# Products with 1/std inside the first projection round, copies on VectorE, and another giving out of the steps between batches

## The chip, the cores and the metric

One core of a Trainium2 chip. The time is device microseconds of one execution of the whole program, the median of three runs of each kernel. One more execution was recorded by the hardware profiler; all durations below come from that one.

## The reference, cut to what matters

Four layers with a residual each act on a field `x` of 4 images, 128 x 128 places, 128 channels, all float32:

```
x = x + L0(gn(x))     # deformable convolution
x = x + L1(gn(x))     # scan over the rows, a 1-d convolution in each step
x = x + L2(gn(x))     # messages
x = x + L3(gn(x))     # triangle multiplication
```

The change concerns the last two. `L2` multiplies every place by `Wself` and adds one term for its row and one for its column. `gn` normalises over groups of 4 channels and all places of an image. `L3` is:

```
xn = layer_norm(x)                                  # over the 128 channels of a place
left  = (xn @ left_w)  * sigmoid(xn @ lgate_w + b)
right = (xn @ right_w) * sigmoid(xn @ rgate_w + b)
out   = einsum('bkjd,bkid->bijd', left, right)      # a 128 x 128 x 128 product per channel
out   = layer_norm(out) * sigmoid(xn @ ogate_w + b)
x     = x + out @ to_out_w + to_out_b
```

## The kernel before, in words

`deform_layer` makes L0, `scan_layer` L1; the field after L1 lies in HBM as `x2T` (channels first). `last_layers` makes L2 and L3 together, batch after batch. It holds one batch at a time in `X`, a tile of 128 channels by 128 x 128 places (64 KB per partition), and one set of projections in `T`, both single. The order of the work is written out by hand: `manual_schedule` keeps, on each of the five engines, the order in which the code emits the instructions, and the parts are Python generators whose steps are interleaved by the loop at L1653. A step is emitted by `step(...)`; `JB` is 8 rows.

For a batch `b` the parts are:

- `messages` (L1333): 16 items. `fetch` loads a tile `x2c` of `x2T` (L1345, SP's queue), POOL adds up the row and column terms (`zc`, L1349); PE multiplies by `ws` (L1363), VectorE adds `zc` and writes `X` transposed (L1368), then takes statistics (L1373). An item is 16 rows by 64 places, so its load has pieces of 64 x 4 = 256 B, and each half of `X` is full after 8 items. The steps of the next batch's messages begin inside the last projection round of the batch before.
- `scaled` (L1379): the group norm's mean and deviation, and eight stores of `X` to HBM as `x3T` (1 MB each, L1394, ACT's queue) for the residual at the end.
- `normed` (L1450): for each of 16 blocks of 8 rows PE centres `X` over the channels into a `pair` of PSUM banks (L1457, two such buffers), ACT squares (L1463), and the centred block is copied back to `X`, by ACT for even blocks (L1468), by VectorE for odd ones (L1470). Every two blocks PE sums the squares (L1491), and a generator `divided` (L1415) takes over: ACT's square root, a trip through HBM (`stdT`) to spread the values over the partitions for a reciprocal, a second trip that loads them spread over all partitions as `rwide` (L1439, two buffers, two loads per block), two products on VectorE (L1446) and a memset of row 0 of `X` to one on POOL (L1447), which carries the bias. Each call of `advance` moves every open `divided` by one step, so a block is multiplied about four double blocks after it was centred, the last ones during the first projection round.
- `multiplied` (L1503), four rounds q = 0 to 3 over 32 of the 128 hidden channels: for each of 16 blocks, 8 matmuls (L1516), a sigmoid on ACT (L1521), two products on VectorE into `T` (L1524), and in every second block an output gate (L1532, L1537, stored to HBM). Then 8 steps of the products over places (L1543, L1547).
- `given_out` (L1553), 40 steps that bring out the batch before: statistics of four columns (L1568), every fourth step their scales with a square root on ACT (L1585), `u` on ACT and POOL (L1632, L1630), transposes (L1602), `y` (L1604, L1605), the residual from `x3T` and the last matmul (L1613, L1617), a copy (L1634) and the store.

The 40 steps are spread over the next batch: 1 ahead of the messages, 3 in them, 4 in `scaled`, 5 in the 25 steps of the norm, 8 in each of the rounds 0 to 2, 3 in round 3. The last batch's steps run alone at the end.

Of the kernel before, what the change touches and what calls it, by code (L numbers as in the profile page):

```python
# [1285 lines left out]
def last_layers(tc, c, terms, w, x2T, out, x3T, gateT, stdT):  # L1286
# [9 lines left out]
    with ExitStack() as ctx:  # L1296
# [36 lines left out]
        def messages(b):  # L1333


            RB, V = 2 * JB, S // 2
            stats = xs[b] = one.tile([P, S // 4, 6], F32, name="stats3")
            todo = [(n, y0) for n in range(2) for y0 in range(0, S, RB)]
            got = []

            def fetch(i):
                if i < len(todo):
                    n, y0 = todo[i]
                    x2c = four.tile([P, RB, V], F32, name="x2c", tag="wide")
                    nc.sync.dma_start(  # L1345
                        x2c, x2T[b, :, y0 : y0 + RB, n * V : (n + 1) * V]
                    )
                    zc = four.tile([P, RB, V], F32, name="zc", tag="wide")
                    nc.gpsimd.tensor_tensor(  # L1349
                        zc, z[:, 0, b, y0 : y0 + RB].unsqueeze(2).to_broadcast([P, RB, V]),  # L1350
                        z[:, 1, b, n * V : (n + 1) * V].unsqueeze(1).to_broadcast([P, RB, V]),
                        ALU.add,
                    )
                    got.append((x2c, zc))

            fetch(0)
            fetch(1)
            yield
            for i, (n, y0) in enumerate(todo):
                x2c, zc = got.pop(0)  # L1360
                pz = pair()
                for h in range(2):
                    nc.tensor.matmul(  # L1363
                        pz[:, h], lhsT=ws[:, b], rhs=x2c[:, JB * h : JB * (h + 1)],
                        start=True, stop=True,
                    )
                x = X[:, n * V : (n + 1) * V]
                nc.vector.tensor_tensor(  # L1368
                    x[:, :, y0 : y0 + RB].rearrange("p w h -> p h w"),
                    pz.rearrange("p n (h w) -> p (n h) w", w=V), zc, ALU.add,  # L1370
                )
                for h in range(2):
                    nc.vector.bn_stats(  # L1373
                        stats[:, 2 * i + h, :], x[:, :, y0 + JB * h : y0 + JB * (h + 1)]
                    )
                fetch(i + 2)
                yield

        def scaled(b):  # L1379

            stats = xs.pop(b)
            mv = two.tile([P, 2], F32, name="mv3")
            nc.vector.bn_aggr(mv, stats.rearrange("p n s -> p (n s)"))
            nc.vector.tensor_tensor(mv[:, 0:1], mv[:, 0:1], w.outb, ALU.subtract)
            mean_ps = single((P, 1))
            nc.tensor.matmul(mean_ps, lhsT=c.gmean, rhs=mv[:, 0:1], start=True, stop=True)
            mean = two.tile([P, 1], F32, name="mean3")
            nc.vector.tensor_copy(mean, mean_ps)
            d = two.tile([P, 1], F32, name="d3")
            nc.vector.tensor_tensor(d, mv[:, 0:1], mean, ALU.subtract)  # L1390
            nc.vector.tensor_tensor(d, d, d, ALU.mult)
            nc.vector.tensor_tensor(d, d, mv[:, 1:2], ALU.add)
            for j0 in range(0, S, 16):
                nc.scalar.dma_start(x3T[b, :, j0 : j0 + 16, :], X[:, j0 : j0 + 16, :])  # L1394
            yield
            var_ps = single((P, 1))
            nc.tensor.matmul(var_ps, lhsT=c.gmean, rhs=d, start=True, stop=True)
            s = two.tile([P, 1], F32, name="s3")
            nc.scalar.activation(s, var_ps, AF.Sqrt, bias=c.eps)
            nc.vector.reciprocal(s, s)  # L1400
            cs = one.tile([P, P], F32, name="cs")
            nc.vector.tensor_scalar(cs, c.center, s, None, ALU.mult)

            shift = two.tile([P, 1], F32, name="shift")
            nc.vector.tensor_tensor(shift, mean, w.outb, ALU.add)
            nc.vector.scalar_tensor_tensor(shift, shift, -1.0, s, ALU.mult, ALU.mult)
            yield
            pc = single((P, 1))
            nc.tensor.matmul(pc, lhsT=c.center, rhs=shift, start=True, stop=True)
            ct = two.tile([P, 1], F32, name="ct")  # L1410
            nc.vector.tensor_copy(ct, pc)
            xs[b] = cs, ct
            yield

        def divided(b, j0, pv):  # L1415

# [11 lines left out]
            nc.vector.reciprocal(rs, rs)  # L1430
            yield
            nc.sync.dma_start(stdT[b, 1, tokens].rearrange("(p e) -> p e", p=P), rs)
            yield
            yield
            for h in range(2):
                rws = []
                for j1 in (j0 + h * JB, j0 + h * JB + 4):
                    rw = two.tile([P, 4 * S], F32, name="rwide")
                    nc.sync.dma_start(  # L1439
                        rw, stdT[b, 1, j1 * S : (j1 + 4) * S].partition_broadcast(P)  # L1440
                    )
                    rws.append((j1, rw))
                yield
                for j1, rw in rws:
                    flat = X[:, j1 : j1 + 4, :].rearrange("p j i -> p (j i)")
                    nc.vector.tensor_tensor(flat, flat, rw, ALU.mult)  # L1446
                nc.gpsimd.memset(X[0:1, j0 + h * JB : j0 + (h + 1) * JB, :], 1.0)  # L1447
            yield

        def normed(b):  # L1450

            cs, ct = xs.pop(b)

            def centred(j1, engine):
                px = pair()
                for n in range(2):
                    nc.tensor.matmul(  # L1457
# [6 lines left out]
                    sq.rearrange("p n e -> p (n e)"), flat, AF.Square, bias=ct  # L1464
                )
                to = X[:, j1 : j1 + JB, :].rearrange("p j i -> p (j i)")
                if engine is nc.scalar:
                    nc.scalar.activation(to, flat, AF.Identity, bias=ct)  # L1468
                else:
                    nc.vector.tensor_scalar(to, flat, ct, None, ALU.add)  # L1470
                return sq

            def advance():
                for d in list(dividing):
                    if next(d, self) is self:
                        dividing.remove(d)

            self = object()
            sqs = [centred(0, nc.scalar)]
            yield  # L1480
            for j0 in range(0, S, 2 * JB):
                sqs.append(centred(j0 + JB, nc.vector))
                advance()
                yield
                if j0 + 2 * JB < S:
                    sqs.append(centred(j0 + 2 * JB, nc.scalar))
                advance()
                yield
                pv = single()
                for q in range(4):  # L1490
                    nc.tensor.matmul(  # L1491
                        pv[32 * q : 32 * q + 32], lhsT=c.mean[:, 0:32],
                        rhs=sqs[q // 2][:, q % 2], start=True, stop=True,
                    )
                del sqs[0:2]
                dividing.append(divided(b, j0, pv))
                advance()
                yield
            while dividing:
                advance()  # L1500
                yield

# [50 lines left out]
        def given_out(b):  # L1553
# [38 lines left out]
            for k in range(-7, NS_ + 1):  # L1592
# [31 lines left out]
                if 0 <= k + 2 < NS_:  # L1624
                    u = us[k + 2] = two.tile([P, 4, P], F32, name="u")
                    for j, (r, m) in enumerate(factors.pop(k + 2)):
                        of = column(b, 4 * (k + 2) + j)
                        to = u[:, j].rearrange("p (q d) -> p q d", q=NQ)
                        if j >= (1 if alone else 4 if k < 6 else 2):
                            nc.gpsimd.tensor_scalar(to, of, r, m, ALU.mult, ALU.add)  # L1630
                        else:
                            nc.scalar.activation(to, of, AF.Identity, bias=m, scale=r)  # L1632
# [8 lines left out]

        order = {getattr(mybir.EngineType, e) for e in ("PE", "Activation", "DVE", "Pool", "SP")}
        ctx.enter_context(tc.manual_schedule(engines=order))
        xs, dividing = {}, []
        END = object()

        def step(of, n=1):
# [4 lines left out]
        out_of = iter(())  # L1652
        for b in range(B):  # L1653

            step(out_of)
            for n, _ in enumerate(msgs):
                if n < 3:
                    step(out_of)
            for n, _ in enumerate(scaled(b)):
                step(out_of, (2, 1, 1)[n])  # L1660
            norm = normed(b)
            for n in range(25):
                step(norm)
                if n in (4, 9, 14, 19, 24):
                    step(out_of)

            msgs = messages(b + 1) if b + 1 < B else iter(())
            for q in range(NQ):
                for n, _ in enumerate(multiplied(b, q)):
                    step(norm)  # L1670
                    if q + 1 < NQ:
                        if n in (1, 3, 5, 7, 9, 11, 15, 20):
                            step(out_of)
                        continue
                    if n in (1, 3, 5):
                        step(out_of)
                    if 7 <= n < 16 or n in (17, 20, 23):
                        step(msgs)
            out_of = given_out(b)
        while step(out_of):  # L1680
# [84 lines left out]
```

## Time and profile before

| | us |
|---|---|
| median of 3 runs (lowest to highest) | 5460.4 (5451.1 to 5470.65) |
| the profiled execution | 5471.3 |
| its span, first to last instruction | 5469.6 |
| PE busy in the span | 4908.4 (90%) |
| DVE busy | 3298.1 (60%) |
| ACT busy | 2491.3 (46%) |
| POOL busy | 1192.2 (22%) |
| `last_layers`, first message item to the end | 3957 to 5470 |
| first q=0 matmul of batches 0 to 3 at | 4082.6, 4402.3, 4758.4, 5113.8 |
| last batch's giving out, alone | 5351 to 5470 |

PE is TensorE's matmuls and PEld its weight loads, DVE is VectorE, ACT ScalarE, POOL GpSimd, SP the engine that issues most DMAs. In a group of the profile the names are `out<-in`, then shapes and the count; then busy time and the mean of one; then the engine's idle time ahead of it and what ended that. A float32 matmul of the code leaves two records.

### The profile page before, as it was taken

To read this page: it belongs to the slowest core of one execution; us is meant where nothing else is said; L and a number is where in the kernel's file an instruction comes from. 1 tells how busy PE (TensorE), PEld (TensorE's weight loads), DVE (VectorE), ACT (ScalarE), POOL (GpSimd) and SP (SyncE) were. 2 spreads that over 40 slices of the span, in tenths; PEclk is the share of its full clock that TensorE was granted. 3 is DMA by queue.
4 is the path that set the end of the run, shared out by engine and by line. 5 is a ranking of instruction groups with operands and counts; after the bars stand their busy time and mean duration, and the time that the engine had idled before them with its cause. 6 is when DMAs were issued, how large, how long until landed. Compare 5 with 4: busy or idle time off the path is not lost. (4 is left out here: it accounts for less than half of the span.)

```text
span 5469.6 us, 162747 instructions
## 1 busy us (share of the span) xinstructions
PE 4908.4 (90%) x68902; PEld 4255.7 (78%) x68902; DVE 3298.1 (60%) x8469; ACT 2491.3 (46%) x5131; POOL 1192.2 (22%) x1097
## 2 busy tenths in 40 slices
PE   1898999999999998989999799999969889798897
PEld 1787788888788787877899799999828478486696
DVE  4676666666566656665555566666654655656545
ACT  1554454544554544544544223323224455563665
POOL 4222121210221201222100011111220233333324
PEclk9999999999998999999999899999989999899998
DMA  5776656665666665655644322222152654646535
GB/s 150 160 160 148 137 133 141 147 151 101 140 139 131 161 120 112 154 121 123 125 91 87 81 82 82 78 78 78 59 156 69 181 169 132 204 152 179 164 130 191
DMA packets 1396696, 710.66 MB, mean 130 GB/s; under 512 B 976717, under 2 KB 1243246, under 8 KB 1386742
## 3 DMA queue, kind: packets, MB, share of 16 engines
q1 hardware_dynamic: 1361810, 625.00, 47.4%
q10 hardware_dynamic: 34148, 75.15, 3.7%
q8 instruction: 545, 8.93, 0.7%
q14 instruction: 193, 1.58, 0.1%
HBM read 417.28 MB, written 282.55 MB: 128 GB/s over the span
## 5 line engine op out<-in xcount | busy, mean ns | idle before, releaser
L606 PE MATMUL conv_ps<-ring,wdef 128*128 128x192 f32 (+2 forms) x7632 | 1297.5, 319 | 8.3 <-DVE x1c L576 5.8
L514 DVE TENSOR_TENSOR m<-t_ps,tent 128x390 f32<-128x390 f32 x1548 | 806.2, 557 | 787.7 <-ACT tent L512 772.2
L606 PEld LDWEIGHTS conv_ps<-ring,wdef 128*128 128x128 f32 x7632 | 1143.3, 195 | 128.0 <-issue 64.8
L512 ACT COPY tent<-t_ps 128x390 f32<-128x390 f32 x1560 | 690.6, 487 | 658.5 <-PE t_ps L498 648.2
L498 PE MATMUL t_ps<-parts_of,spread 57*64 57x99 bf16 (+1 forms) x12384 | 742.6, 275 | 169.8 <-DVE m L514 147.8
L523 PE MATMUL v_ps<-m,pixels 60*64 60x108 f32 (+1 forms) x22704 | 813.8, 264 | 17.6 <-DVE m L514 8.2
L498 PEld LDWEIGHTS <-spread 57*64 57x64 bf16 x12480 | 578.5, 125 | 314.5 <-issue 267.1
L523 PEld LDWEIGHTS v_ps<-m,pixels 60*64 60x64 f32 x22704 | 674.0, 137 | 68.9 <-DVE m L514 22.6
L549 ACT COPY ring<-v_ps 128x432 f32<-128x432 f32 x1032 | 505.0, 525 | 442.6 <-PE v_ps L523 441.9
L420 POOL TENSOR_TENSOR off<-off,koff 72x512 f32<-72x512 f32 x128 | 162.6, 1271 | 1766.8 <-DVE off L417 1766.8
L1516 PEld LDWEIGHTS pair_ps<-wcat,X 128*128 128x128 f32 x4096 | 482.1, 195 | 64.1 <-issue 37.2
L1516 PE MATMUL pair_ps<-wcat,X 128*128 128x128 f32 x4096 | 492.9, 279 | 23.8 <-DVE T L1524 12.3
L1112 PEld LDWEIGHTS own_ps<-diff,wconv 128*128 128x128 f32 x4064 | 494.1, 191 | 13.2
L1524 DVE TENSOR_TENSOR T<-pair_ps,sig 128x256 f32<-128x256 f32 x512 | 280.5, 592 | 370.3 <-ACT sig L1521 370.3
L1112 PE MATMUL own_ps<-diff,wconv 128*128 128x128 f32 x4064 | 494.9, 273 | 0.0
L506 PE MATMUL t_ps<-parts_of,spread 57*64 57x130 bf16 x9288 | 454.9, 225 | 0.6 <-issue 0.6
L1152 POOL TENSOR_TENSOR sum_h<-sum_h,x2c 128x512 f32<-128x512 f32 x128 | 162.7, 1271 | 1142.7 <-DVE x2c L1138 689.7
L438 DVE SCALAR_TENSOR_TENSOR parts<-off,parts 72x512 bf16<-72x512 f32 x384 | 296.1, 772 | 154.0 <-ACT parts L430 148.2
L1068 ACT ACTIVATE rowT<-x1T_ps,t_x,s_x 128x128 f32<-128x128 f32 x512 | 207.4, 566 | 309.9 <-PE x1T_ps L1064 292.5
L506 PEld LDWEIGHTS <-spread 57*64 57x64 bf16 x9312 | 319.5, 108 | 0.6 <-issue 0.5
L1521 ACT ACTIVATE sig<-pair_ps 128x512 f32<-128x512 f32 x256 | 151.2, 597 | 317.1 <-PE pair_ps L1516 201.1
L1101 PE MATMUL both_ps<-carry,wsum 128*128 128x128 f32 x2032 | 269.2, 274 | 1.1 <-DVE carry L1135 1.1
(196 smaller groups left out, 6712.2 us busy)
## 6 DMA issues: line engine op xcount, KB each, us to landing
pixels<-tab SPq DMA_DIRECT2D x688, 123.8 KB
parts_of<-off SPq DMA_DIRECT2D x1032, 55.7 KB
off<-parts SPq DMA_DIRECT2D x64, 891.0 KB
tab<-rows SPq DMA_DIRECT2D x384, 128.0 KB
xin<-in_x_dram SPq DMA_DIRECT2D x128, 256.0 KB
x<-x1c SPq DMA_DIRECT2D x32, 1024.0 KB
x1rows<-x SPq DMA_DIRECT2D x128, 256.0 KB
x2T<-x2c ACTq DMA_DIRECT2D x128, 256.0 KB
```

Source lines behind the costliest of these rows:

```text
L438: nc.vector.scalar_tensor_tensor(parts[:, NSPLIT + i, h : h + RO, 2 : S + 2], off, 0.0, part, ALU.is_gt, ALU.mult,)
L498: nc.tensor.matmul(tp[h : h + HALF, 0, 0:n].rearrange("p (r c) -> p r c", c=PADW)[:, :, i:PADW:RX], lhsT=spread[0:k, kx // 2, i, h : h + H ...
L506: nc.tensor.matmul(tp[h : h + HALF, 1, i * PADW : (i + 1) * PADW], lhsT=spread[HALF : HALF + k, kx // 2, first + i, h : h + HALF], rhs=src ...
L512: nc.scalar.copy(tent[:, 0:n], tp[:, 0, 0:n])
L514: nc.vector.tensor_tensor(m, *pair, ALU.mult)
L523: nc.tensor.matmul(to[p1 : p1 + HALF], lhsT=pix[p0 : p0 + LANES, xb, :], rhs=m[p0 : p0 + LANES, :, RX * xb : RX * xb + w], start=True, sto ...
L549: nc.scalar.copy(to, bodies[side])
L606: nc.tensor.matmul(pc[:, at : at + rows, x0:x1], lhsT=wdef[:, side, k, :], rhs=v[:, :, k if v.shape[2] == NK else kx, x0 + kx : x1 + kx], ...
L1101: nc.tensor.matmul(both, lhsT=wsum[:, j, :], rhs=old[h][:, 1, :, j : j + V], start=(j == 0), stop=(j == NJ - 1),)
L1112: nc.tensor.matmul(own[:, n], lhsT=wt[:, 2 * j + n, :], rhs=diffs[h][:, n, :, j : j + V], start=False, stop=(n == 1 and j == NJ - 1),)
L1516: nc.tensor.matmul(pj[:, j], lhsT=X[:, j0 + j, :], rhs=w.wcat[:, q * 4 * DQ : (q + 1) * 4 * DQ], start=True, stop=True,)
L1524: nc.vector.tensor_tensor(to, pj[:, :, e].rearrange("p j d -> p d j"), sig[:, :, e].rearrange("p j d -> p d j"), ALU.mult,)
```

## The change

Six edits, all in `last_layers`:

1. `messages`: for batch 0 `parts` is 1, so an item is 8 rows by 128 places (pieces of 4 KB). The other batches keep 16 rows by 64.
2. The first half of `X` is stored to `x3T` from SP's queue in step 9 of `messages` for batches 1 to 3; `scaled` stores only the second half there, and the whole for batch 0.
3. `divided` becomes `inverted`, which ends when 1/std is in HBM. The spreading loads and the products are now plain functions, `spread` and `divide`. The loop calls them for block 0 ahead of the first round, and then in the first round, after block n of the projections is emitted: the product of block n+1, then the load for block n+2.
4. All 16 copies of centred blocks are on VectorE.
5. `u` of the first steps of giving out (k < 6) is shared with POOL as in the later ones.
6. The 40 steps are given out anew: 2 in the messages, 5 in `scaled`, 12 in the norm, 7, 7, 6 and 2 in the four rounds. The next batch's messages have 13 steps in round 3 instead of 12.

```diff
@@ messages
-            RB, V = 2 * JB, S // 2
+            parts = 2 if b else 1
+            RB, V = JB * parts, S // parts
+            RH = RB // 2
...
-            todo = [(n, y0) for n in range(2) for y0 in range(0, S, RB)]
+            todo = [(n, y0) for n in range(parts) for y0 in range(0, S, RB)]
...
                 fetch(i + 2)
+                if b and i == len(todo) // 2 + 1:
+                    for j0 in range(0, S // 2, 16):
+                        nc.sync.dma_start(x3T[b, :, j0 : j0 + 16, :], X[:, j0 : j0 + 16, :])
                 yield
@@ scaled
-            for j0 in range(0, S, 16):
+            for j0 in range(S // 2 if b else 0, S, 16):
                 nc.scalar.dma_start(x3T[b, :, j0 : j0 + 16, :], X[:, j0 : j0 + 16, :])
@@ divided -> inverted, spread, divide
             nc.sync.dma_start(stdT[b, 1, tokens].rearrange("(p e) -> p e", p=P), rs)
-            yield
-            yield
-            for h in range(2):
-                rws = []
-                for j1 in (j0 + h * JB, j0 + h * JB + 4):
-                    rw = two.tile([P, 4 * S], F32, name="rwide")
-                    nc.sync.dma_start(
-                        rw, stdT[b, 1, j1 * S : (j1 + 4) * S].partition_broadcast(P)
-                    )
-                    rws.append((j1, rw))
-                yield
-                for j1, rw in rws:
-                    flat = X[:, j1 : j1 + 4, :].rearrange("p j i -> p (j i)")
-                    nc.vector.tensor_tensor(flat, flat, rw, ALU.mult)
-                nc.gpsimd.memset(X[0:1, j0 + h * JB : j0 + (h + 1) * JB, :], 1.0)
-            yield
+
+        def spread(b, j0):
+
+            for j1 in (j0, j0 + 4):
+                rw = two.tile([P, 4 * S], F32, name="rwide")
+                nc.sync.dma_start(rw, stdT[b, 1, j1 * S : (j1 + 4) * S].partition_broadcast(P))
+                spreads.append((j1, rw))
+
+        def divide():
+
+            j0 = spreads[0][0]
+            for j1, rw in spreads:
+                flat = X[:, j1 : j1 + 4, :].rearrange("p j i -> p (j i)")
+                nc.vector.tensor_tensor(flat, flat, rw, ALU.mult)
+            spreads.clear()
+            nc.gpsimd.memset(X[0:1, j0 : j0 + JB, :], 1.0)
@@ normed
-                if engine is nc.scalar:
-                    nc.scalar.activation(to, flat, AF.Identity, bias=ct)
-                else:
-                    nc.vector.tensor_scalar(to, flat, ct, None, ALU.add)
+                nc.vector.tensor_scalar(to, flat, ct, None, ALU.add)
@@ given_out
-                        if j >= (1 if alone else 4 if k < 6 else 2):
+                        if j >= (1 if alone else 2):
@@ the loop over the batches
-            step(out_of)
             for n, _ in enumerate(msgs):
-                if n < 3:
+                if n % 2:
                     step(out_of)
             for n, _ in enumerate(scaled(b)):
-                step(out_of, (2, 1, 1)[n])
+                step(out_of, (2, 2, 1)[n])
             norm = normed(b)
             for n in range(25):
                 step(norm)
-                if n in (4, 9, 14, 19, 24):
+                if n % 2:
                     step(out_of)
+            spread(b, 0)
+            divide()
+            spread(b, JB)
 
             msgs = messages(b + 1) if b + 1 < B else iter(())
             for q in range(NQ):
+                beside = (
+                    (1, 4, 7, 10, 13, 15, 20), (1, 4, 7, 10, 13, 15, 20),
+                    (1, 4, 7, 11, 15, 20), (9, 12),
+                )[q]
                 for n, _ in enumerate(multiplied(b, q)):
-                    step(norm)
-                    if q + 1 < NQ:
-                        if n in (1, 3, 5, 7, 9, 11, 15, 20):
-                            step(out_of)
-                        continue
-                    if n in (1, 3, 5):
+                    if q == 0:
+                        step(norm)
+                        if n + 1 < S // JB:
+                            divide()
+                        if n + 2 < S // JB:
+                            spread(b, (n + 2) * JB)
+                    if n in beside:
                         step(out_of)
-                    if 7 <= n < 16 or n in (17, 20, 23):
+                    if q + 1 == NQ and (7 <= n < 16 or n in (16, 18, 20, 22)):
                         step(msgs)
```

More of the change, by code (lines that the diff above doesn't have):

```diff
@@ L1363, in messages @@
                     nc.tensor.matmul(
-                        pz[:, h], lhsT=ws[:, b], rhs=x2c[:, JB * h : JB * (h + 1)],
+                        pz[:, h], lhsT=ws[:, b], rhs=x2c[:, RH * h : RH * (h + 1)],
                         start=True, stop=True,
@@ L1373, in messages @@
                     nc.vector.bn_stats(
-                        stats[:, 2 * i + h, :], x[:, :, y0 + JB * h : y0 + JB * (h + 1)]
+                        stats[:, 2 * i + h, :], x[:, :, y0 + RH * h : y0 + RH * (h + 1)]
                     )
                 fetch(i + 2)
+                if b and i == len(todo) // 2 + 1:
+                    for j0 in range(0, S // 2, 16):
+                        nc.sync.dma_start(x3T[b, :, j0 : j0 + 16, :], X[:, j0 : j0 + 16, :])
                 yield
@@ L1413, in scaled, with inverted @@
             yield
-        def divided(b, j0, pv):
+        def inverted(b, j0, pv):
             std = three.tile([P, 512], F32, name="std", tag="gate")
@@ L1432, in divided, with centred @@
             nc.sync.dma_start(stdT[b, 1, tokens].rearrange("(p e) -> p e", p=P), rs)
-            yield
-            yield
-            for h in range(2):
-                rws = []
-                for j1 in (j0 + h * JB, j0 + h * JB + 4):
-                    rw = two.tile([P, 4 * S], F32, name="rwide")
-                    nc.sync.dma_start(
-                        rw, stdT[b, 1, j1 * S : (j1 + 4) * S].partition_broadcast(P)
-                    )
-                    rws.append((j1, rw))
-                yield
-                for j1, rw in rws:
-                    flat = X[:, j1 : j1 + 4, :].rearrange("p j i -> p (j i)")
-                    nc.vector.tensor_tensor(flat, flat, rw, ALU.mult)
-                nc.gpsimd.memset(X[0:1, j0 + h * JB : j0 + (h + 1) * JB, :], 1.0)
-            yield
+        def spread(b, j0):
[10 more added lines that the diff above has]
+            nc.gpsimd.memset(X[0:1, j0 : j0 + JB, :], 1.0)
         def normed(b):
             cs, ct = xs.pop(b)
-            def centred(j1, engine):
+            def centred(j1):
                 px = pair()
@@ L1466, in centred @@
                 to = X[:, j1 : j1 + JB, :].rearrange("p j i -> p (j i)")
-                if engine is nc.scalar:
-                    nc.scalar.activation(to, flat, AF.Identity, bias=ct)
-                else:
-                    nc.vector.tensor_scalar(to, flat, ct, None, ALU.add)
+                nc.vector.tensor_scalar(to, flat, ct, None, ALU.add)
                 return sq
             def advance():
-                for d in list(dividing):
+                for d in list(inverting):
                     if next(d, self) is self:
-                        dividing.remove(d)
+                        inverting.remove(d)
             self = object()
-            sqs = [centred(0, nc.scalar)]
+            sqs = [centred(0)]
             yield
             for j0 in range(0, S, 2 * JB):
-                sqs.append(centred(j0 + JB, nc.vector))
+                sqs.append(centred(j0 + JB))
                 advance()
@@ L1485, in normed @@
                 if j0 + 2 * JB < S:
-                    sqs.append(centred(j0 + 2 * JB, nc.scalar))
+                    sqs.append(centred(j0 + 2 * JB))
                 advance()
@@ L1495, in normed @@
                 del sqs[0:2]
-                dividing.append(divided(b, j0, pv))
+                inverting.append(inverted(b, j0, pv))
                 advance()
                 yield
-            while dividing:
+            while inverting:
                 advance()
@@ L1643, in last_layers @@
         ctx.enter_context(tc.manual_schedule(engines=order))
-        xs, dividing = {}, []
+        xs, inverting, spreads = {}, [], []
         END = object()
```

## The prediction, made before the changed kernel ran

> **What bounds the kernel now.** I read the page first, then the busy time by stage, then the groups of instructions, then the timeline of one stage. The change touches only `last_layers`, the last 1,512 us of the span (3957 to 5470 us). In it four batches run one after the other, each through the same stages, so I asked for the busy time of each engine stage by stage. The columns are: stage, its length, busy us (and instructions) of PE, PEld, DVE, ACT, POOL, the granted TensorE clock, the DMA share and GB/s.
>
> ```profile
> core 0: us, PE busy (x) PEld busy (x) DVE busy (x) ACT busy (x) POOL busy (x), PEclk, DMA share, GB/s
> 4039.00:4082.60 43.60, 40.77 (x130) 13.72 (x130) 16.45 (x22) 29.90 (x31) 4.71 (x5) 0.94 0.33 116
> 4082.60:4128.00 45.40, 33.58 (x206) 27.90 (x204) 26.47 (x47) 12.40 (x20) 9.41 (x10) 0.85 0.49 150
> 4147.00:4191.00 44.00, 43.01 (x340) 38.83 (x339) 17.67 (x32) 19.15 (x33) 0.00 (x0) 1.00 0.13 49
> 4299.00:4336.00 37.00, 18.45 (x47) 8.74 (x47) 32.79 (x74) 8.60 (x17) 10.79 (x7) 0.79 0.89 294
> 4336.00:4402.00 66.00, 54.17 (x211) 24.10 (x210) 28.10 (x53) 46.07 (x65) 12.82 (x13) 0.86 0.44 141
> 4402.00:4474.00 72.00, 63.90 (x472) 58.03 (x471) 42.34 (x98) 42.52 (x73) 28.39 (x33) 0.92 0.60 185
> 4474.00:4533.00 59.00, 57.12 (x465) 52.61 (x465) 30.46 (x76) 40.95 (x71) 18.89 (x24) 1.00 0.43 143
> ```
>
> Rows 1 to 3 are batch 0: its norm, most of its first projection round (q=0), and its second (q=1). Rows 4 to 7 are batch 1: the end of its messages with the scales, norm, q=0, q=1. Where PE has nothing to wait for (q=1) it is busy at full clock: a round without giving out takes 44 us, with 8 steps of giving out 59, so a step costs PE (59.1-43.9)/8 = 1.9 us, the price of a step on a full PE. PE has holes in three places: the end of the messages (18 of 37 us busy, DVE 33: DVE bounds it), the norm (54 of 66) and q=0 (64 of 72). Batches 2 and 3 repeat this: norm and q=0 together take 137.1, 134.0 and 135.9 us, from the first matmul of L1457 to the last of L1543. The holes of a batch come to about 40 us; that is all a better order can win in it.
>
> The pieces of a projection round are these groups (mean ns of one before the bar's end):
>
> ```profile
> L1516 PE MATMUL pair_ps<-wcat,X 128*128 128x128 f32 x4096 | 492.9, 279 | 23.8 <-DVE T L1524 12.3 <-POOL X L1447 6.3 <-DVE X L1470 5.1
> L1524 DVE TENSOR_TENSOR T<-pair_ps,sig 128x256 f32<-128x256 f32 x512 | 280.5, 592 | 370.3 <-ACT sig L1521 370.3
> L1521 ACT ACTIVATE sig<-pair_ps 128x512 f32<-128x512 f32 x256 | 151.2, 597 | 317.1 <-PE pair_ps L1516 201.1 <-DVE T L1524 81.2 <-ACT x L1634 30.0
> L1446 DVE TENSOR_TENSOR X<-X,rwide 128x512 f32<-128x512 f32 x128 | 86.7, 695 | 88.3 <-DMA rwide<-stdT 87.8
> L1447 POOL MEMSET X<- 1x1024 f32 x64 | 60.3, 942 | 251.6 <-DVE X L1446 222.8 <-issue 9.9 <-ACT gate L1537 7.2
> ```
>
> The product with 1/std (L1446) waits 88 us for its spread rows, but it runs some blocks ahead of the projections, so most of this is hidden. The timeline of batch 1's q=0 shows the links from one block to the next, and one of batch 0 what a gap does to PE:
>
> ```profile
> 4410.66 0.60 ACT L1521 ACTIVATE sig<-pair_ps 128x512 f32<-128x512 f32 x1 [0.83 <-ACT x L1634]
> 4411.29 1.11 DVE L1524 TENSOR_TENSOR T<-pair_ps,sig 128x256 f32<-128x256 f32 x2 [1.42 <-ACT sig L1521]
> 4412.32 1.37 DVE L1446 TENSOR_TENSOR X<-X,rwide 128x512 f32<-128x512 f32 x2
> ```
>
> ```profile
> 4382.14 1.33 DVE L1446 TENSOR_TENSOR X<-X,rwide 128x512 f32<-128x512 f32 x2 [2.67 <-DMA rwide<-stdT]
> 4383.53 0.94 POOL L1447 MEMSET X<- 1x1024 f32 x1 [3.22 <-DVE X L1446]
> ```
>
> ```profile
> 4089.73 3.49 PEld L1516 LDWEIGHTS pair_ps<-wcat,X 128*128 128x128 f32 x16 [5.31 <-POOL X L1447]
> ```
>
> DVE takes its instructions in the order of the code: the T products of a block (L1524), then the next L1446. A block's 16 matmul records take 1.87 us when blocks follow each other (two in 3.74 us at 4408.63), 2.03 us to the start of its sigmoid, but 3.5 us in the last line, after PE had stood for 5.3 us behind a memset.
>
> **The Trainium skill.** "TensorE: Matmul & The Clock Gate", section "HAM oscillation": gaps of more than about 3.4 us send the array back to half clock. The trace agrees: L1516 records have a median of 275 ns in a full PE and 421 ns after that gap of 5.3 us. "DMA: Bandwidth & Descriptors", "Specifications": pieces under 512 B don't reach line rate. It agrees: x2c (512 KB in pieces of 256 B) lands some 4.4 us after issue with no store beside it, while x3T (1 MB in pieces of 8 KB) lands every 2.5 us. The same page, "Queues, rings and completion order": a DMA engine takes the descriptors of one issuing queue in ring order. The trace has only the case with two queues: an x2c load issued at 3996.8 us, just behind four x3T stores on ACT's queue, landed after 13.9 us.
>
> **The change, part by part** (sums against the profiled execution, 5471.3 us with a span of 5469.6; it lies 10.9 us over the median of 5460.4).
>
> *Products moved into q=0.* In the new loop `divide()` for block n+1 stands after the whole of block n of `multiplied`. On DVE it is therefore behind T(n), which waits for sigmoid(n), which waits for the matmuls of block n; and the matmuls of block n+1 wait for the product and for the memset of row 0. That is a closed chain, once per block: matmuls to sigmoid 2.03 + sigmoid 0.60 + 0.03 + T products up to the next DVE start 1.03 + product 1.33 + 0.06 + memset 0.94 + about 0.05 = **6.07 us**. At half clock the first link is 3.6, and the chain 7.7 us. PE has 1.87 us in it, plus 0.86 for a gate matmul in every second block, plus 2 us where giving out stands. So PE is 40% (batch 0) to 50% full, and some matmuls will run at half clock. I take 6.6 us for batches 1 to 3, where giving out fills six of the gaps, and 7.1 for batch 0, where nothing does. Other work in the gap is hidden: the stats of giving out (1.2 us on DVE) stand behind the product, in the 3.5 us of memset, matmuls and sigmoid; POOL's y and u (2.5 us) stand behind the memset and end before the next. The new spread has two `rwide` buffers for two DMAs, so it starts when the previous product ends; the second lands about 3.0 us after that (batch 0: cycle of 4.05 us per block, of which 1.3 is product), before the 4.7 us that the chain leaves. The square root in `scales` isn't hidden: twice in q=0 ACT does it, u, x and a table load (1.28) ahead of the sigmoid, about 2.25 us late, 4.5 in all. The first spread has nothing ahead of it but the norm: landing, product and memset, 3.5 us.
> Batch 0: 3.5 + 16 x 7.1 + 7.4 (second half of the round, as at 4139.5 to 4146.9) = 124.5 against 64.3 us: **+60**.
> Batches 1 to 3: q=0 is 3.5 + 16 x 6.6 + 4.5 + 7.4 + 2 (one step of giving out there) = 123.
>
> *Norm with twelve steps and DVE copies.* PE per two blocks: 2 x 1.88 + 1.06 + 1.5 steps x 2.05 = 7.9 us, 63 in all. DVE has 16 copies of 1.28 instead of 8 (+10 us) and loses about 11 us of products; ACT loses 8 x 1.11. The copy still waits for the square of the same bank, so a pair buffer is held 1.88 + 1.12 + 1.28 + 0.1 = 4.4 us, 2.2 per block with two buffers; this fits in 7.9 per two. I take 67 us (63 to 72) where 5 steps took 62.5 to 66. Norm and q=0: 190 against 135.7, **+54** per batch. Batch 0 has no giving out; its norm stays at 43.6.
>
> *Giving out taken from elsewhere.* q=1 has 7 steps instead of 8 (-1.9), q=2 6 (-3.5), q=3 none on PE but one item of messages more (-1; batch 3, without messages, -3).
>
> *End of messages, batches 1 to 3.* One item of 3.2 us and two steps' stats fewer on DVE (-5 to -6), scales -3 since PE meets fewer transposes. Against it: four x3T stores (10 us of data) now stand on SP's queue ahead of the last four x2c loads, and hold the next by about 9 us, of which DVE's lag hides some 4. Net **-5** (-9 to +2). POOL's two u for k<6 take load from ACT: nothing, since neither bounds here.
>
> *Batch 0's rows whole.* X is written from 3969.4 to 4032.7, 3.96 us per item; DVE alone needs 1.91 + 2 x 0.685 = 3.2. With 4 KB pieces, and without the x3T stores in the middle, DVE bounds: -12. No row shows the new stride; if it costs, 0. All eight x3T stores now come after the last item, and ACT's square root behind their issue (7.8 instead of 3.1 us): +3. Their data (20 us) runs ahead of the norm's writes.
>
> Sum: batch 0 +60 - 12 + 3 = +51; batches 1 to 3: +54 - 1.9 - 3.5 - 1 - 5 = +43 each, 129; batch 3's last round -2. Together **+178**: 5649 for a profiled run, less 10.9: **5640 us** for the median.
>
> **Rivals.** (1) The chain isn't closed, because products run ahead as before; then q=0 takes PE's own 2.4 (batch 0) to 3.1 us per block. In the sum above the block's time C enters as -252 + 64C, so it turns at C = 3.9 us. 16 x 2.4 + 48 x 3.1 = 187 gives -65: **5395 us**, faster. For it: nothing else in the stage needs more than 3.1 us. Against it: L1446 directly follows L1524 on DVE in the timeline, in code order.
> (2) The spread, not the chain, bounds: SP serves stores of gates, x3 and gate loads in order, and was held 2.3 us at one such place (4409.7 to 4412.0). If each spread came 2.5 us later than I take, the slack of 1.7 is gone and a block costs about 1.4 more: 64 x 1.4 = 90, **5730 us**. Against it: the spread is issued ahead of the step's DMAs.
> (3) Gains and losses cancel, C near 4: **5460 us**.
>
> **How the numbers follow.** Chances: forecast 0.80, rival 1 0.08, rival 2 0.09, rival 3 0.03. Bounds around the forecast: C from 6.07 everywhere (-42) to 7.7 in batch 0 and 7.3 elsewhere (+43); norm -12 to +15; messages -12 to +21 and, in batch 0, up to +12. Taken as independent about 55 either way; I reach a little further down, since half clock is the least certain: **5570 to 5700**. About 0.3% (16 us) is what a measurement of this kernel can tell from no change: faster 0.08, same 0.03, slower 0.89.
>
> **What would show it.** Batch periods of about 398 us instead of 355; L1524 waiting for the sigmoid in every block of q=0; PE's longest idle in the stage ended by POOL's memset; TensorE clock near 0.75 there. Batch 0's messages near 52 us. It is wrong if blocks of q=0 follow in under 4 us, or if L1446 still waits for rwide in most blocks.

## The result, and the profile after

The changed kernel takes **5695.15 us** (median of 4, 5692.24 to 5719.15) against 5455.75 us for the kernel before in the same comparison: ratio **1.0447, 95% interval 1.0408 to 1.0487**, 239 us slower by the medians. The profiled execution has a span of 5692.4 us, against 5469.6.

By the first matmul of the messages, `last_layers` begins at 3952.7 us (before: 3965.4). The code ahead of it is the same in both; from run to run this start moved between 3953 and 3975 us, and the giving out of the last batch at the end took 110 to 121 us without an edit to it. So the stages, not the whole time, are compared below. They are marked by the records of the trace: messages end with the last write of `X`, `scaled` with the first centring matmul, the norm with the last sum of squares, the lead with the first projection, each round with its last product over places. In us:

```
             messages scaled  norm  lead   q=0   q=1   q=2   q=3   batch
before, b=0     67.3    6.2   43.7  -0.1   64.3  43.9  43.9  63.9  333.1
before, b=1     25.3   12.6   62.4   3.4   71.4  59.1  57.6  67.5  359.4
before, b=2     25.3   12.6   59.9   2.6   71.4  59.1  57.6  67.1  355.7
before, b=3     25.3   12.4   60.3   2.2   73.3  59.1  57.6  47.0  337.3
after,  b=0     54.0   10.0   41.3   7.5  126.8  43.9  43.9  67.9  395.1
after,  b=1     26.9   11.1   64.3   7.4  125.2  61.5  52.8  68.1  417.1
after,  b=2     26.4   11.1   64.1   6.7  127.9  59.7  52.8  68.1  416.8
after,  b=3     25.7   11.1   64.3   7.4  125.2  61.4  52.8  43.9  391.8
```

The batches together are 235 us longer, and q=0 alone 225. The busy time by stage of the changed kernel, with the columns as in the prediction, for batch 0's norm, q=0 and q=1, then batch 1's end of messages, scales, norm, lead, the blocks of q=0 and q=1:

```profile
core 0: us, PE busy (x) PEld busy (x) DVE busy (x) ACT busy (x) POOL busy (x), PEclk, DMA share, GB/s
4016.60:4065.40 48.80, 40.62 (x130) 13.52 (x130) 22.97 (x25) 23.87 (x25) 0.94 (x1) 0.92 0.31 112
4065.40:4182.70 117.30, 65.44 (x271) 54.72 (x272) 34.41 (x62) 13.15 (x22) 17.85 (x17) 0.67 0.25 82
4192.00:4236.00 44.00, 43.01 (x340) 38.83 (x339) 17.70 (x32) 19.02 (x32) 0.00 (x0) 1.00 0.13 48
4347.80:4374.70 26.90, 11.51 (x17) 4.47 (x16) 14.77 (x17) 0.59 (x1) 5.71 (x3) 0.75 0.78 221
4374.70:4385.80 11.10, 2.45 (x11) 2.37 (x12) 9.61 (x36) 2.87 (x5) 1.21 (x2) 0.56 0.91 378
4385.80:4450.00 64.20, 61.61 (x321) 34.54 (x320) 39.79 (x94) 49.37 (x77) 28.45 (x36) 0.97 0.42 129
4450.00:4457.40 7.40, 0.05 (x4) 0.00 (x0) 2.02 (x5) 2.29 (x3) 3.28 (x4) 0.81 0.57 173
4457.40:4574.00 116.60, 67.85 (x372) 58.87 (x373) 47.48 (x100) 32.68 (x53) 26.44 (x31) 0.79 0.39 125
4582.60:4644.10 61.50, 57.16 (x451) 52.51 (x450) 28.04 (x68) 37.78 (x65) 16.65 (x21) 0.97 0.38 125
```

The norm is now what one would wish: PE is busy for 61.6 of 64.2 us, with twelve steps of giving out in it. In the blocks of batch 0's q=0 no engine is busy for more than 56% of the time, and the array runs at 0.67 of its clock: that fits a closed chain, though the table alone doesn't show one. PE's 65 busy us there are themselves long because of the clock. The same groups as in the prediction:

```profile
L1518 PE MATMUL pair_ps<-wcat,X 128*128 128x128 f32 x4096 | 562.0, 300 | 240.2 <-POOL X L1453 226.9 <-DVE T L1526 13.2
L1526 DVE TENSOR_TENSOR T<-pair_ps,sig 128x256 f32<-128x256 f32 x512 | 281.0, 591 | 630.3 <-ACT sig L1523 630.3
L1523 ACT ACTIVATE sig<-pair_ps 128x512 f32<-128x512 f32 x256 | 152.7, 597 | 600.1 <-PE pair_ps L1518 499.6 <-DVE T L1526 72.8 <-ACT x L1636 19.9
L1451 DVE TENSOR_TENSOR X<-X,rwide 128x512 f32<-128x512 f32 x128 | 82.1, 681 | 16.9 <-DMA rwide<-stdT 16.9
L1453 POOL MEMSET X<- 1x1024 f32 x64 | 60.3, 942 | 426.4 <-DVE X L1451 426.4
```

Busy times hardly moved, except PE's (493 to 562 us, a record's mean from 279 to 300 ns). The waits did: PE waited 24 us ahead of the projections before, 240 now, 227 of them ended by POOL's memset. The product's own wait for its spread rows fell from 88 to 17. The waits of batch 1's q=0 (who waits, for whom: us in total, times, longest) close the circle. The step from T to the next product isn't among them, since it is no wait but VectorE's own order:

```profile
POOL X L1453 <- DVE X L1451: 88.2, 16, 7.0
ACT sig L1523 <- PE pair_ps L1518: 68.6, 12, 7.7
DVE T L1526 <- ACT sig L1523: 63.7, 15, 5.6
PE pair_ps L1518 <- POOL X L1453: 56.1, 16, 7.4
```

Each of the four waits for the one before it in the chain, in 12 to 16 of the 16 blocks. None of these rows alone is a cause: a reader who stops at the third would blame the sigmoid, at the fourth the memset. In the timeline of batch 0 one turn of the chain reads (lines of other work left out):

```profile
4097.63 0.60 ACT L1523 ACTIVATE sig<-pair_ps 128x512 f32<-128x512 f32 x1 [4.44 <-PE pair_ps L1518]
4098.26 1.07 DVE L1526 TENSOR_TENSOR T<-pair_ps,sig 128x256 f32<-128x256 f32 x2 [4.41 <-ACT sig L1523]
4099.41 1.23 DVE L1451 TENSOR_TENSOR X<-X,rwide 128x512 f32<-128x512 f32 x2
4100.69 0.94 POOL L1453 MEMSET X<- 1x1024 f32 x1 [5.84 <-DVE X L1451]
4101.69 3.78 PE L1518 MATMUL pair_ps<-wcat,X 128*128 128x128 f32 x16 [4.15 <-POOL X L1453]
```

### The profile page after: what moved, and what is told of

Its sections match the earlier page's. It is cut to its first block, busy times and chain, and to the rows that moved or that the text cites. A ratio compares the mean times of both kernels' runs of the same rounds, so it can differ in the third digit from the quotient of the medians.

```text
span 5692.4 us, 162705 instructions
## 1 busy us (share of the span) xinstructions
PE 4957.5 (87%) x68902; PEld 4302.1 (76%) x68902; DVE 3330.4 (59%) x8501; ACT 2434.7 (43%) x5045; POOL 1218.4 (21%) x1145
## 5 line engine op out<-in xcount | busy, mean ns | idle before, releaser
L1518 PEld LDWEIGHTS pair_ps<-wcat,X 128*128 128x128 f32 x4096 | 540.6, 213 | 315.0 <-POOL X L1453 260.0
L1518 PE MATMUL pair_ps<-wcat,X 128*128 128x128 f32 x4096 | 562.0, 300 | 240.2 <-POOL X L1453 226.9
```

The source lines that it names most:

```text
L1518: nc.tensor.matmul(pj[:, j], lhsT=X[:, j0 + j, :], rhs=w.wcat[:, q * 4 * DQ : (q + 1) * 4 * DQ], start=True, stop=True,)
```

## The experiments

Ratios are to the kernel before, run on the same chip as the experiment. "Block" is the mean distance of the 16 blocks of q=0 from first matmul to first matmul, in the profiled execution; a block is called cold where the median of its L1518 records is over 400 ns (it is 421 ns then and 275 in a warm one; over the cold block at 4101.7 us the granted clock was 0.50). In the changed kernel the four batches have blocks of 7.57, 7.35, 7.44 and 7.35 us (6.09 at the shortest), and 14, 8, 9 and 8 cold ones; in the kernel before 3.5 to 3.9 us, and one or two cold ones.

**Products one block further ahead.** Edit to the changed kernel:

```diff
             spread(b, 0)
             divide()
             spread(b, JB)
+            divide()
+            spread(b, 2 * JB)
...
-                        if n + 1 < S // JB:
+                        if n + 2 < S // JB:
                             divide()
-                        if n + 2 < S // JB:
-                            spread(b, (n + 2) * JB)
+                        if n + 3 < S // JB:
+                            spread(b, (n + 3) * JB)
```

> The changed kernel with the products of q=0 one block further ahead: block n+2 is multiplied after block n is projected, so VectorE has the product of block n+1 behind it when it comes to the T products of block n. Closed chain (my theory): the chain is cut; what is left is the product (1.33 us) and its spread with two buffers (3.0 us), 4.35 us a block instead of 7.4 to 7.6. That is 64 x 3 = about -190 us: 5500 us (5470 to 5540). Rival, the spread or SP's queue sets the pace: blocks stay over 6.5 us, 5640 to 5700. Rival, the cost lies in the twelve steps within the norm: unchanged, 5690.

Measured: 5546.47 us, ratio 1.0142 (1.0112 to 1.0173). Blocks of 4.15, 4.85, 4.83 and 4.91 us; q=0 takes 74.8 us in batch 0 and 90 to 93 in the others. PE, VectorE, ACT and POOL have as many instructions as before; what differs is where the products, with their memsets and spreads, stand in the order. Some 160 us came back, less than the 190 expected, since blocks in batches 1 to 3 take 4.8 to 4.9 rather than 4.35. The waits in batch 0's q=0 show that the limit has changed hands:

```profile
DVE X L1451 <- DMA rwide<-stdT: 28.4, 25, 4.4
DVE T L1526 <- ACT sig L1523: 3.2, 3, 1.8
```

VectorE now waits for the spread rows 25 times in its 32 products, and for the sigmoid hardly at all.

**Memset twice.** Edit to the changed kernel:

```diff
-            nc.gpsimd.memset(X[0:1, j0 : j0 + JB, :], 1.0)
+            for _ in range(2):
+                nc.gpsimd.memset(X[0:1, j0 : j0 + JB, :], 1.0)
```

> The changed kernel with the memset of row 0 issued twice for each block of q=0. If the chain is closed and POOL's memset a link of it, each of the 64 blocks grows by one memset (0.94 us and the step to the next instruction): +62 us, ratio 1.056 (1.052 to 1.059), a block at 7.1 us with a warm array and 8.8 with a cold one. If the memset has slack (POOL is 21% busy), the time stays at ratio 1.0447.

Measured: 5784.34 us, ratio 1.0571 (1.0539 to 1.0602). The shortest blocks of batches 1 to 3 are 7.09 us, against 6.09: the whole memset stands in the chain. The means are 8.73 to 8.81 us. In batches 1 to 3, 12 or 13 of 16 blocks are cold, against 8 or 9, so the longer gap also cost clock there. (Batch 0 has 16 cold ones; that says little, since a kernel below with the unchanged loop, the one with the stores behind the last load, has 16 there too.) POOL's 21% of busy time says nothing about the memset's place in the chain.

**Filler matmuls.** Edit to the changed kernel:

```diff
                     if n in beside:
                         step(out_of)
+                    elif q == 0 and n < S // JB:
+                        pf = single()
+                        for j in range(10):
+                            nc.tensor.matmul(
+                                pf[:, 0:P], lhsT=X[:, n * JB + j % JB, :],
+                                rhs=w.wcat[:, 0 : 4 * DQ], start=True, stop=True,
+                            )
```

> The changed kernel with ten matmuls whose result nobody reads in each gap of q=0 that has no step of giving out (2.3 us at full clock, in a gap of 4). If half clock is what makes a block 7.8 instead of 6.1 us, about 14 blocks of batch 0 and 8 to 10 of each other batch win 1.7 us: -70 us, 5625 us (5610 to 5650), with L1518's records at 275 ns in nearly all blocks. If the clock isn't the cause, the added work delays the chain or changes nothing: 5695 to 5760.

Measured: 5673.06 us, ratio 1.0372 (1.0344 to 1.0401): 41 us less than the changed kernel by the ratios (1.0447 less 1.0372, of 5464), where 70 were expected. Blocks took 6.75 us in batch 0 and about 6.95 in the others. Cold blocks fell to 6, 4, 4 and 4. The six of batch 0 are the first block and the five that follow a gap which the edit leaves empty, because a step of giving out has its place there and batch 0 has none. All ten blocks behind a filled gap are warm. Three records (L1689 is the filler) show an empty gap and then a filled one:

```profile
4121.00 3.78 PE L1518 MATMUL pair_ps<-wcat,X 128*128 128x128 f32 x16 [4.14 <-POOL X L1453]
4126.28 2.70 PE L1689 MATMUL one_ps<-wcat,X 128*128 128x128 f32 x20
4128.85 2.05 PE L1518 MATMUL pair_ps<-wcat,X 128*128 128x128 f32 x16
```

In the other batches the four are the first block, one behind a step of giving out, and the two behind the long blocks with the square root of `scales`, where 5.1 us stayed idle in spite of the filler. The kernel does more and ends earlier, so half clock is a part of the price; the chain's 6.1 us stay in every warm block.

**Four buffers for the spread rows.** On top of the kernel with products one block further ahead; the two halves of a block now share one 4 KB buffer of the kind that x2c, zc and the squares use, and four spreads stand ahead of the round instead of three:

```diff
-                rw = two.tile([P, 4 * S], F32, name="rwide")
+            both = four.tile([P, 2, 4 * S], F32, name="rwide", tag="wide")
...
-                        if n + 3 < S // JB:
-                            spread(b, (n + 3) * JB)
+                        if n + 4 < S // JB:
+                            spread(b, (n + 4) * JB)
```

> The products one block further ahead, as in the run of that name with two buffers, and the spread rows in the four 4 KB buffers that x2c, zc and the squares use at other times, so that up to four blocks of them are under way. If the spread with its two buffers (4.2 us a block in batch 0) is what was left of q=0's length, blocks now follow in 2.4 to 3.1 us: q=0 near 50 us in batch 0 and 62 in the others, against 75 and 91: about -115 us more, 5430 us (5410 to 5460), ratio 0.994. If PE's order and POOL's memset hold it: 5500 to 5540, ratio over 1.007.

Measured: 5479.01 us, ratio 1.0031 (1.002 to 1.0043). Blocks of 3.18 us in batch 0 and 3.92 to 3.95 in the others, q=0 58.9 and 77 to 78 us. The spread was the limit left, and of the 1.0447 it leaves 1.0031; but I expected 2.4 to 3.1 us a block, and 0.994. Most of the last 0.8 us of a block in batches 1 to 3 is in two places: a block of 9.4 us, in which a sigmoid waits behind the square root of `scales` and its table load, and the block behind it, cold, of 5.6 to 6.2 us. Without these two the mean is 3.36 us. What holds those 3.36 was not taken apart.

**x3T stores back on ACT's queue.** The changed kernel without the four stores in `messages`, with all eight in `scaled`.

> The changed kernel with all eight x3T stores of each batch issued in scaled from ACT's queue, as before. If the four stores on SP's queue hold the loads of x2c behind them, VectorE's wait of 11 us per batch 1 to 3 goes, less some 1.5 us for ACT's longer issue: -28 us, 5667 us (5655 to 5680). If VectorE bounds there anyway: 5690 to 5700.

Measured: 5707.59 us, ratio 1.0434 (1.0405 to 1.0463): no gain that can be told from none. The messages' end takes 24.9 to 25.1 us instead of 25.7 to 26.9. Its waits there are those of the changed kernel over again:

```profile
PE pair_ps L1365 <- DMA x2c<-x2T: 12.1, 2, 10.7
DVE X L1370 <- PE pair_ps L1365: 10.1, 1, 10.1
```

```profile
4363.46 27.96 ACTq L1396 DMA_DIRECT2D x3T<-X  x8
```

ACT reaches the stores at 4363.5 us, right after its last copy of q=3, and issues the first four while the last loads of x2c are still to come. In the kernel before, ACT stood at a square root of the giving out until 4318.2 us, by which time the last load had landed; that accident protected it. My theory of the queue was wrong: the wait is the same behind stores on either queue. The next run tests whether it is their data.

**x3T stores behind the last load.** Edit to the changed kernel:

```diff
-                if b and i == len(todo) // 2 + 1:
+                if b and i == len(todo) - 3:
```

> The changed kernel with the four x3T stores of the first half of X placed after the last x2c load has been issued (step 13 of messages instead of 9), still on SP's queue. The run with the stores back on ACT's queue kept the wait, since ACT came to them just as early. If it is the stores' data ahead of the last loads that costs 10 us, on whichever queue, it goes in batches 1 to 3: -31 us, ratio 1.039, messages' end 16 us instead of 26. If the wait only moves (into the norm's writes or the loads of the residual): ratio 1.0435 to 1.045.

Measured: 5673.58 us, ratio 1.0379 (1.035 to 1.0408). The messages' end takes 14.7, 14.7 and 14.8 us instead of 26.9, 26.4 and 25.7; `scaled` gives 2 to 3 us of it back (13.0 to 14.5). PE's wait for the loads in batch 1 falls from 12.0 us to:

```profile
PE pair_ps L1365 <- DMA x2c<-x2T: 3.7, 3, 1.5
```

So the four stores ahead of the loads cost the changed kernel some 9 us in each of three batches. The ratios alone, whose intervals meet at 1.0408, would hardly tell; the stages do.

**The giving out alone.** The kernel before with edits 4, 5 and 6, and its own `divided`.

> The kernel before with only the copies on VectorE, u shared with POOL from the start and the steps given out anew (12 in the norm, 13 steps of messages in q=3); products, stores and loads as before. My theory says that these parts alone are a gain: norm +6, q=0 -2, elsewhere -6.4, end of messages and scales -8 in batches 1 to 3, together -30: 5425 us (5405 to 5450). If the twelve steps within the norm are themselves a part of the loss: 5480 to 5550.

Measured: 5486.73 us, ratio 1.0032 (1.0016 to 1.0048): a small loss where I expected a gain. The norm takes 72.4 to 76.2 us instead of 60 to 62, and 50.1 instead of 43.7 in batch 0: with the products still in the norm, twelve steps there instead of five, and all copies on VectorE, it got longer. No engine is full in it (in batch 1 PE is busy for 63 of 72 us, VectorE for 51, ACT for 50), and which wait holds it was not taken apart. The messages' end gained nothing (25.0), for the reason just shown: with the steps given out anew, ACT issues the stores early (from 4309.5 us in batch 1), and PE waits 12.2 us for two loads.

**Whole rows alone.** The kernel before with the first edit.

> The kernel before with the first edit alone: batch 0's items of 8 whole rows. By the stages of the changed kernel its messages take 54 instead of 67 us and scaled 10 instead of 6.2: -10 us, 5454 us, ratio 0.998. If the gain was given back at the end of the batch: ratio 1.000.

Measured: 5448.3 us, ratio 0.9975 (0.9965 to 0.9985). Batch 0's messages take 52.8 us instead of 67.3, `scaled` 10.0 instead of 6.2, as expected. This part of the change is a gain.

**Joined.** The kernel with four buffers, with the stores behind the last load, and with the first spreads and products inside the norm instead of behind it:

```diff
             for n in range(25):
                 step(norm)
+                if n in (21, 22):
+                    spread(b, (n - 21) * JB)
+                if n > 22:
+                    divide()
+                    spread(b, (n - 21) * JB)
```

> All that the runs point to: the changed kernel with the products one block further ahead, four buffers for the spread rows, the first two spreads and products within the norm's last four steps, and the x3T stores behind the last x2c load. Theory: as with four buffers (5430), less 31 for the stores and about 24 for the 7 us between norm and first projection: 5385 us (5360 to 5420), ratio 0.986. If the parts hinder each other: 5430 or more.

Measured: 5442.84 us, ratio 0.9963 (0.995 to 0.9977), against 0.986 expected. The batches take 322.6, 355.5, 356.4 and 331.1 us (before: 333.1, 359.4, 355.7, 337.3). The lead fell from about 7 to 2.5 us in batches 1 to 3, the end of messages to 14.8; but q=0 takes 78 to 80 us there, where 62 were expected, and that is the missing part. Four blocks, the first two, the one with the square root of `scales` and the one behind it, take 25 to 28 of the 61 to 63 us from the first block to the last. It is faster than the kernel before; whether it is faster than whole rows alone, the intervals (0.995 to 0.9977 and 0.9965 to 0.9985) don't tell.

## Why the prediction was right, and where its sum was short

The direction and the mechanism were right: 5640 us was forecast, 5695 measured, within 5570 to 5700, but only just: the interval of the ratio, 5678 to 5721 us, reaches past the range. The table gives 235 us for the four batches where the working had 178, a quarter short. By its steps:

- **The closed chain: right.** Most warm blocks take 6.09 to 6.13 us, predicted 6.07. Cold ones take 7.5 to 7.9 (7.84 from 4132.4 to 4140.3 us), predicted 7.7. Moving the product one place ahead removes most of the loss, and doubling a link adds that link to the block. Rival 1 (products run ahead as before) needed blocks under 3.9 us and is refuted. So is rival 2: apart from the first, no product of batch 0's q=0 waits for its spread rows, and this is the only such wait there:

```profile
DVE X L1451 <- DMA rwide<-stdT: 4.4, 1, 4.4
```

- **The share of cold blocks: too low.** I took 7.1 us a block for batch 0; with 14 of 16 cold it is 7.57. For batches 1 to 3 I took 6.6 and, apart, 4.5 us for the two square roots of `scales`. The blocks with these last 9.4 us, so each adds 3.3 rather than 2.25; 8 or 9 cold blocks make up the rest of 7.35 to 7.44. With its second half and without the lead q=0 came to 125 to 128 us instead of 119.5 in batches 1 to 3, and to 126.8 instead of 121 in batch 0.
- **The lead: 3.5 predicted, 6.7 to 7.5 measured.** I wrote that the first spread has nothing ahead of it but the norm, and gave landing, product and memset 3.5 us together. The product and the memset take 2.4 of these, so I had left about 1 us for the way through HBM. In batch 1, where the norm's last sum of squares ends at 4450.0 us:

```profile
4449.66 0.32 SPq L1437 DMA_DIRECT2D stdT<-rstd  x1
4450.31 0.61 SPq L1432 DMA_DIRECT2D rstd<-stdT  x1
4450.98 5.74 SPq L1443 DMA_DIRECT2D rwide<-stdT  x4
4455.02 1.35 DVE L1451 TENSOR_TENSOR X<-X,rwide 128x512 f32<-128x512 f32 x2 [4.36 <-DMA rwide<-stdT]
```

  SP comes to the spread 1.0 us after the norm's end, behind the DMAs of a later `inverted`; the product starts 4.0 us after that; product, memset and the steps between them take 2.4. In batch 0, where no giving out stands beside it, the same parts are 1.3, 3.5 and 2.7 us. So it is mostly the landing that I had too short, and SP's order does the rest. Where the first spreads are issued inside the norm (the joined kernel), the lead is 2.5 us in batches 1 to 3.
- **The norm: 67 predicted, 64.1 to 64.3 measured.** With the products gone PE is full. Batch 0's 43.6 became 41.3.
- **The end of messages and the scales: -5 predicted, about 0 measured.** This was the term with the wrong reasoning. I let VectorE's lag hide 4 of 9 us; the profile shows PE waiting 12.0 us for two loads, and VectorE 10.9 us in one piece for PE:

```profile
DVE X L1370 <- PE pair_ps L1365: 12.2, 3, 10.9
PE pair_ps L1365 <- DMA x2c<-x2T: 12.0, 2, 9.5
```

  Nothing was hidden, and it isn't SP's queue in particular, as the run with ACT's queue showed.
- **Batch 0's messages: -12 + 3 predicted, -13.3 + 3.8 measured.** The new stride of the writes costs nothing visible.
- **Giving out elsewhere.** q=2 became 4.8 us shorter (3.5 predicted), but q=1 0.6 to 2.4 us longer instead of 1.9 shorter: in the changed kernel PE has a gap of 3.0 us there in batch 1, at 4601 us, where the square root of `scales` and two table loads of 1.28 us hold a sigmoid. In batch 0, q=3 grew by 4.0 us for its additional item of messages, which the sum left out.

Together: batch 0 has +62 for +51, batches 1 to 3 +58, +61 and +55 for +43, +43 and +41.

## What to carry to other kernels

Before moving a step into a loop, write down for one turn of the loop what each engine has ahead of it in its own order; where the step's result is needed by the next turn and its place in the order is behind this turn's result, the loop has become serial, and its time is the sum of the links and no longer the busiest engine's share. One turn more of distance cuts the chain at no cost in instructions; here it took the ratio from 1.0447 to 1.0142, and more buffers for what it needs took it to 1.0031. And a table of busy shares doesn't show such a chain: look for a circle of waits in which every engine waits for the one before.

## What the runs showed of the hardware that I had not expected

The clock's loss feeds on the chain. In the changed kernel's q=0, by PE's longest idle time between two blocks, each of the 26 blocks behind 3.9 us or more was cold, and each of the 20 behind less than 2.5 us was warm. Behind 2.6 to 3.2 us 9 were cold and 5 warm, so the 3.4 us that the prediction quotes isn't the line that separates them here. Three kernels with the same loop had 14, 15 and 16 cold blocks of 16 in batch 0. Ten matmuls for nothing (2.3 us at full clock) in a gap kept the next block of batch 0 warm ten times of ten, while all five behind an empty gap were cold.

Four stores of 1 MB ahead of a load hold it up on whichever queue they are issued: x2c landed 12.3 us after its issue behind stores on SP's queue (the changed kernel), and 13.9 us behind stores on ACT's (the kernel before, batch 0), where it takes some 4.4 us with no store beside it. That is 8 to 9.5 us more, nearly all of the 10 us that the stores' data take.
